# A scan kernel whose tiles hold four channel chunks side by side instead of two, with the products after the scan cut by tokens instead of by chunk pairs

## The chip, the cores and the metric

The kernel runs on one core of a Trainium2 chip. The metric is device time in microseconds (us): the median of several executions. Each profile is one execution, with its own time. The engines are named as in the profile: PE (matmuls and transposes), PEld (its weight loads), ACT (ScalarE), DVE (VectorE), POOL (GpSimd), SP (SyncE, which only issues DMAs here). Every engine works through its own queue in order; semaphores join them.

## The reference: what is computed

The input `x` is 8 x 1024 tokens of 256 features. Three blocks follow each other, each with a residual: half an FP4-quantized gated FFN, a Mamba block, and the same FFN once more.

```
x = x + 0.5 * ffn(layernorm(x))
x = x + mamba(layernorm(x))
x = x + 0.5 * ffn(layernorm(x))
```

The Mamba block is where the change lies. 512 inner channels, 16 states, one recurrence along the tokens for each channel and state:

```
dA = exp(delta[..., None] * A)                    # tokens x 512 x 16
dBu = delta[..., None] * Bm[:, :, None, :] * u[..., None]
h[t] = dA[t] * h[t-1] + dBu[t]
y[t] = sum over states n of h[t, :, n] * Cm[t, n]  ; y = y + u * D
out = (y * silu(z)) @ out_proj_w
```

## The kernel before, in words

The 8192 tokens are cut into 16 chunks of 512 tokens, two to each of the 8 sequences. For a chunk, channels lie on the 128 partitions (four channel chunks, `dc` = 0 to 3) and tokens along the row. Stages: FFN 1 (`stage_f1`), the projections and the convolution (`stage_m1`), the gate z (`stage_z`), the scan over 16 states (`scan`), and the output with FFN 2 (`stage_out`). Several chunks are in work at a time.

**The scan** (`scan_step`, lines 863 to 883). For each state k, ACT makes four tiles `s_bu` (L874) and four tiles `s_da` = exp(delta*A) (L878). PE turns `s_bu` into channel order in PSUM (`s_pb`, L881). DVE runs four scans of 512 tokens (L883), each of which writes one channel chunk into the tile `s_h` (128 x 2048, float32). In chunks that are the first of their sequence, ACT then saves the last token's state (`s_carry`, L908), for the sequence's second chunk; there the scans start from it.

**The layout.** `s_h` is seen through `pairs` (line 528): two halves, each with 512 tokens of two channel chunks that alternate, `(a t q)` with q = 2. So a scan writes every second word of its half. The product with C (`times_c`, L888) runs on POOL in two instructions for each state, one for each half: it multiplies 128 x 1024 elements of `s_h` in place by the row `s_cbc`, in which each value of C is repeated for the two channel chunks of its token (step 0 in the last dimension). In the last chunk's last two states the second of the two runs on DVE.

**The sum over states** is made by DMA: POOL adds each `s_h` to one of two buffers in HBM, `accd` (L920, even and odd states); `accd` starts from u*D, which ACT writes as `m_ud` (L802) in the same layout. At the end of a chunk the buffers are added to the last `s_h` (L914, L915) and POOL multiplies by silu(z) (L852): it reads `s_h` with a step of two words and writes `m_sz`, one instruction for each pair of channel chunks. PE's output projection (L857) follows. In the last chunk the buffers are loaded into `o_y` instead (L835, L836), DVE adds the last two `s_h` (L850) and does the product itself.

**What sets the order.** The program first writes down all instructions, then `set_order` builds a graph of their dependencies, prices them with a table (`price`), searches for a good order on every engine, and pins it. A changed dependency therefore moves instructions everywhere, not just at the place of the edit. `s_h` has five buffers, which `m_ud` and the last chunk's `f_ht` share.

Of the kernel before, what the change touches and what calls it, by code (L numbers as in the profile page):

```python
# [11 lines left out]
F32 = mybir.dt.float32  # L12
BF16 = mybir.dt.bfloat16
I32 = mybir.dt.int32
AF = mybir.ActivationFunctionType
ALU = mybir.AluOpType
# [5 lines left out]
P = 128  # L22
T = 512
# [14 lines left out]
KS = 1  # L38
KE = 1
W_T = ((0.01, 0.08, 0.085), (0.02, 0.09, 0.095), (0.15, 0.25, 0.3), 0.2)  # L40

BE = (0,)
CE = (0,)
BUFS = {
    'accd': 4, 'bcol': 2, 'big': 1, 'bu': 7, 'carry': 2, 'cbc': 2, 'cd': 4, 'da': 4, 'delta': 2,
# [17 lines left out]
ND = DI // P  # L63
# [364 lines left out]
def macaron(ctx: ExitStack, tc: tile.TileContext, x_in, norm_w, norm_b, in_w, conv_w,  # L428
            conv_b, xp_w, dt_w, dt_b, a_log, d_par, out_w, w_gate, w_up, w_down, out):
    nc = tc.nc  # L430
    NB, L, _ = x_in.shape
    chunks = []
    for b in range(NB):
        t = 0
# [23 lines left out]
    dr = ctx.enter_context(tc.tile_pool(name="dr", bufs=3, space=DRAM))  # L458
    sb, psq, psb, dr = Pool(sb), Pool(psq), Pool(psb), Pool(dr)
    pools = [Pool(q) for q in pools]  # L460

    def pst(shape, name):
        turn[kind[0]] += 1
        i = PSM[kind[0]][turn[kind[0]] % len(PSM[kind[0]])]
        t = pools[i].tile([P, 512], F32, tag=f"ps{i}", name=name)
        n = 1
        for k in shape[1:]:
            n *= k
        v = t[: shape[0], :n]
        if len(shape) == 3:  # L470
            v = v.rearrange("p (a b) -> p a b", a=shape[1])
        return v
# [14 lines left out]
    def cload(shape, src, name):  # L487
        t = const.tile(shape, F32, name=name)
        loads.append((t, src))
        return t  # L490
# [3 lines left out]
    def eng(what):  # L494
        return getattr(nc, ENG[what])
# [15 lines left out]
    dh = cload([P, ND], d_par.rearrange("(c p) -> p c", p=P), "dh")  # L511
# [14 lines left out]
        nc.vector.tensor_scalar(an, an, -1.0, None, ALU.mult)  # L526
        yield

    def pairs(h, n):

        return h.rearrange("p (a t q) -> p a t q", a=ND // 2, q=2)[:, :, :n, :]


    def quant(v, n, floor, mul0, mul1):
# [162 lines left out]
    x1d, accd, szd, cd = {}, {}, {}, {}  # L697
    duT, delta, bcol = {}, {}, {}
    carry = {}
# [3 lines left out]
    def tok(ap, s):  # L703
        b, t0, n = chunks[s]
        return ap[b, t0 : t0 + n, :].rearrange("(t p) d -> p t d", p=P)
# [11 lines left out]
    def stage_m1(s):  # L717
        n = chunks[s][2]
        nt = n // P
# [14 lines left out]
        for pr in range(nt // 2):  # L734
# [4 lines left out]
            for j in range(2):  # L739
                t = 2 * pr + j  # L740
                b, r = stats[t]
# [8 lines left out]
        u2 = sb.tile([P, ND, T], F32, tag="big", bufs=BUFS["big"], name="m_u2")  # L750
# [29 lines left out]
        pb = pst([P, nt, P], "m_pb")  # L780
# [12 lines left out]
        nc.scalar.activation(dl, dl, AF.Softplus)  # L793
        yield

        accd[s] = dr.tile([2, P, ND // 2, 2 * T], F32, tag="accd", bufs=BUFS["accd"], name="accd")
        ud = pairs(sb.tile([P, ND * T], F32, tag="h", bufs=BUFS["h"], name="m_ud"), n)
        dg = 1 if fine else DG
        for d0 in range(0, ND, dg):
            d1 = slice(d0, d0 + dg)  # L800
            for dc in range(d0, d0 + dg):
                nc.scalar.activation(ud[:, dc // 2, :, dc % 2], u2[:, dc, :n], AF.Copy, scale=dh[:, dc : dc + 1])  # L802
            eng('du').tensor_tensor(u2[:, d1, :n], u2[:, d1, :n], dl[:, d1], ALU.mult)
        nc.sync.dma_start(accd[s][0], ud.rearrange("p a t q -> p a (t q)"))
        yield
        duT[s] = []
        for t in range(nt):
# [22 lines left out]
    y_of, last_h = {}, {}  # L830

    def load_y(s):
        y = pairs(sb.tile([P, ND * T], F32, tag="big", bufs=BUFS["big"], name="o_y"), chunks[s][2])
        yf = y.rearrange("p a t q -> p a (t q)")
        nc.sync.dma_start(yf, accd[s][0])  # L835
        nc.gpsimd.dma_start(yf, accd[s][1], accum_op=ALU.add)  # L836
        return y

    def stage_out(s):
        n = chunks[s][2]  # L840
        nt = n // P
        muls = (eng('hx'), eng('hq')) if s < S - ENDV else (nc.vector, nc.vector)
        x4 = sb.tile([P, NT, DM], F32, tag="x4", bufs=BUFS["x4"], name="x4b")
        nc.sync.dma_start(x4[:, :nt], x1d[s][:, :nt])
        y, sz = y_of.pop(s), szd[s]

        for a in range(ND // 2):
            if s in last_h:
                for h in last_h[s]:
                    nc.vector.tensor_tensor(y[:, a], y[:, a], h[:, a], ALU.add)  # L850
            zv = sz[:, 2 * a : 2 * a + 2, :]
            (eng('y') if s < S - KE else nc.vector).tensor_tensor(zv, y[:, a].rearrange("p t q -> p q t"), zv, ALU.mult)  # L852
        yield
        for t in range(nt):
            po = pst([P, DM], "o_po")
            for dc in range(ND):
                nc.tensor.matmul(po, sz[:, dc, t * P : (t + 1) * P], outw[:, dc, :], start=(dc == 0), stop=(dc == ND - 1))  # L857
            nc.vector.tensor_tensor(x4[:, t, :], x4[:, t, :], po, ALU.add)
        yield
        yield from ffn(x4, nt, muls, s >= S - KE)  # L860
        nc.sync.dma_start(tok(out, s), x4[:, :nt])

    def scan_step(s, k, h):
        n = chunks[s][2]
        nt = n // P
        first = chunks[s][1] == 0
        bu_v = BE[S - 1 - s] if S - 1 - s < len(BE) else 0
        bu = []
        for t in range(nt):
            b = sb.tile([P, DI], F32, tag="bu", bufs=BUFS["bu"], name="s_bu")  # L870
            if t * bu_v % nt < bu_v:
                nc.vector.tensor_scalar(b, duT[s][t], bcol[s][:, t, k : k + 1], None, ALU.mult)
            else:
                nc.scalar.activation(b, duT[s][t], AF.Copy, scale=bcol[s][:, t, k : k + 1])  # L874
            bu.append(b)
        for dc in range(ND):
            da = sb.tile([P, T], F32, tag="da", bufs=BUFS["da"], name="s_da")[:, :n]
            nc.scalar.activation(da, delta[s][dc], AF.Exp, scale=an[:, dc, k : k + 1])  # L878
            pb = psb.tile([P, T], F32, tag="psb", name="s_pb")[:, :n]
            for t in range(nt):  # L880
                nc.tensor.transpose(pb[:, t * P : (t + 1) * P], bu[t][:, dc * P : (dc + 1) * P], ident)  # L881
            init = 0.0 if first else carry[chunks[s][0]][:, k, dc : dc + 1]
            nc.vector.tensor_tensor_scan(h[:, dc // 2, :, dc % 2], da, pb, init, ALU.mult, ALU.add)  # L883

    def times_c(s, k, h, cbc):
        last = s >= S - KE and k >= NS - 2
        for a in range(ND // 2):
            (nc.vector if last and a else nc.gpsimd).tensor_tensor(  # L888
                h[:, a], h[:, a], cbc.unsqueeze(2).to_broadcast([P, chunks[s][2], 2]), ALU.mult)

    def scan(s):
        n = chunks[s][2]
        if chunks[s][1] == 0:

            carry[chunks[s][0]] = sb.tile([P, NS, ND], F32, tag="carry", bufs=BUFS["carry"], name="s_carry")
        for k in range(0, NS, 2):
            cbc = sb.tile([P, 2, T], F32, tag="cbc", bufs=BUFS["cbc"], name="s_cbc")[:, :, :n]
            nc.sync.dma_start(cbc, cd[s][0:1, k * n : (k + 2) * n].rearrange("o (a t) -> o a t", a=2)
                              .partition_broadcast(P))
            if s >= S - KE and k == NS - 2:  # L900
                y_of[s] = load_y(s)
            last = s >= S - KE and k == NS - 2
            for j in range(2):
                h = pairs(sb.tile([P, ND * T], F32, tag="h", bufs=BUFS["h"], name="s_h"), n)
                hf = h.rearrange("p a t q -> p a (t q)")
                scan_step(s, k + j, h)
                if chunks[s][1] + n < L:
                    nc.scalar.activation(carry[chunks[s][0]][:, k + j].rearrange("p (a q) -> p a q", q=2), h[:, :, n - 1, :], AF.Copy)  # L908
                times_c(s, k + j, h, cbc[:, j, :])
                if last:  # L910
                    last_h.setdefault(s, []).append(h)
                elif k + j == NS - 1:

                    nc.gpsimd.dma_start(hf, accd[s][1], accum_op=ALU.add)  # L914
                    nc.gpsimd.dma_start(hf, accd[s][0], accum_op=ALU.add)  # L915
                    y_of[s] = h
                elif k + j == 1:
                    nc.sync.dma_start(accd[s][1], hf)
                else:
                    nc.gpsimd.dma_start(accd[s][j], hf, accum_op=ALU.add)  # L920
                yield


# [55 lines left out]
```

## Time and profile before

| | us |
|---|---|
| median of three executions | 2452.26 (2449.67 to 2452.42) |
| the profiled execution, its time | 2451.14 |
| its span in the profile | 2449.0 |
| PE busy (clock granted: 0.99 on average) | 2341.7, 96% of the span |
| DVE busy | 2177.9, 89% |
| ACT busy | 2142.2, 87% |
| POOL busy | 2064.2, 84% |

In the profile a busy time is the union of an engine's instructions; matmuls are pipelined and their ends are modelled, so PE's 96% is not PE at its peak. A row of the groups names line, engine, operation, tiles, shapes and count, then busy time and the mean duration of one in ns, then the idle time just ahead of these instructions and what ended most of it. The chain of waits follows the work back from the last instruction, at each step to what released it.

### The profile page before, as it was taken

What the parts mean: (1) busy time and instruction counts of PE and PEld (TensorE: products, weight loads), DVE (VectorE), ACT (ScalarE), POOL (GpSimd) and SP (SyncE); (2) the same over time, 40 slices, a digit from 0 to 9 for tenths busy, and PEclk for the clock granted to TensorE, in tenths of its full rate; (3) what the DMA queues carried; (4) which work ended last, traced back from release to release, by engine and by line L of the source; (5) the groups of instructions that cost most, each with busy time, mean ns of one, the idle gap of its engine ahead of it and who ended that gap; (6) DMA issues with size and microseconds to landing.
All of it is one profiled execution on the core that took longest, in us unless ns stands there. A gap on an engine that the chain in (4) does not pass through costs nothing.

```text
span 2449.0 us, 33713 instructions
## 1 busy us (share of the span) xinstructions
PE 2341.7 (96%) x11260; PEld 1617.9 (66%) x11260; DVE 2177.9 (89%) x3074; ACT 2142.2 (87%) x3952; POOL 2064.2 (84%) x1554
## 2 busy tenths in 40 slices
PE   7989999999999999999999999999999999998888
PEld 5566666667676666666667666666667666655556
DVE  7569898998989899898999889898998989888995
ACT  4489898999989998998999899898998999999852
POOL 4358898899989999898897999899898999888972
PEclk8999999999999999999999999999999999999899
DMA  3049888787877888598886978889787888899970
GB/s 94 18 115 192 192 166 197 166 200 170 165 191 168 203 185 187 138 185 193 175 196 140 210 169 171 189 173 208 167 178 174 179 190 191 189 211 199 198 149 18
DMA packets 90461, 416.28 MB, mean 170 GB/s; under 512 B 12016, under 2 KB 30320, under 8 KB 53552
## 3 DMA queue, kind: packets, MB, share of 16 engines
q0 software_dynamic: 36576, 266.35, 57.6%
q1 hardware_dynamic: 53712, 147.78, 18.4%
q8 instruction: 88, 1.44, 0.2%
q14 instruction: 85, 0.70, 0.1%
HBM read 129.42 MB, written 284.69 MB: 169 GB/s over the span
## 4 chain that ended last, share of the span: by engine, by line
PE 59%; ACT 13%; POOL 11%; DVE 8%; issue 4%; DMA 3%; SPq 0%; POOLq 0%; DVEq 0%; ACTq 0%
PE s_pb L881 11%; PE f_po L662 9%; PE f_pg L642 9%; PE f_pu L642 8%; PE m_pc L765 6%; POOL s_h L888 5%; DVE s_h L883 4%; ACT s_bu L874 4%; PE m_px L755 3%; ACT s_da L878 3%; PE m_pz L823 3%; PE o_po L857 2%; PE m_pp L775 2%; PE m_pd L791 2%; DMA s_h<-accd 2%
## 5 line engine op out<-in xcount | busy, mean ns | idle before, releaser
L888 POOL TENSOR_TENSOR s_h<-s_h,s_cbc 128x1024 f32<-128x1024 f32 x510 | 1136.9, 2270 | 125.0 <-ACT s_carry L908 71.0
L878 ACT ACTIVATE s_da<-m_delta,an 128x512 f32<-128x512 f32 x1024 | 720.7, 718 | 35.3 <-DVE s_h L883 33.5
L881 PEld LDWEIGHTS s_pb<-ident,s_bu 128*128 128x128 f32 x4096 | 505.3, 142 | 335.6 <-issue 132.5
L874 ACT ACTIVATE s_bu<-m_duT,m_bc 128x512 f32<-128x512 f32 x1024 | 701.4, 717 | 12.5 <-PE s_pb L881 9.9
L881 PE MATMUL s_pb<-ident,s_bu 128*128 128x128 f32 x4096 | 652.3, 277 | 44.7 <-DVE s_h L883 34.4
L883 DVE TENSOR_TENSOR_SCAN s_h<-s_da,s_carry,s_pb 128x512 f32<-128x512 f32 x512 | 638.3, 1264 | 22.2 <-PE s_pb L881 18.9
L883 DVE TENSOR_TENSOR_SCAN s_h<-s_da,s_pb 128x512 f32<-128x512 f32 x512 | 608.5, 1206 | 27.3 <-PE s_pb L881 20.2
L662 PE MATMUL f_po<-wdn,f_ht 128*128 128x256 f32 x1536 | 395.3, 382 | 10.0 <-ACT f_ht L659 7.8
L642 PE MATMUL f_pg<-wg,f_xt 128*128 128x352 f32 x1024 | 365.4, 465 | 4.4 <-ACT f_xt L632 1.8
L642 PE MATMUL f_pu<-wu,f_xt 128*128 128x352 f32 x1024 | 360.3, 463 | 5.2 <-DVE f_h L646 3.2
L662 PEld LDWEIGHTS f_po<-wdn,f_ht 128*128 128x128 f32 x1536 | 270.0, 190 | 76.2 <-issue 22.7
L765 PE MATMUL m_pc<-m_xp,cdg 128*128 128x512 f32 x512 | 253.4, 596 | 1.9 <-ACT m_car L762 1.8
L552 POOL TENSOR_TENSOR f_h<-f_h,q_sc 128x704 f32<-128x704 f32 x128 | 195.9, 1534 | 50.8 <-DVE f_h L551 46.2
L642 PEld LDWEIGHTS f_pu<-wu,f_xt 128*128 128x128 f32 x1024 | 177.6, 191 | 89.5 <-issue 21.7
L920 POOL DMA_DIRECT2D accd<-s_h x223 | 209.6, 940 | 26.3 <-POOL s_h L888 18.0
L642 PEld LDWEIGHTS f_pg<-wg,f_xt 128*128 128x128 f32 x1024 | 176.0, 191 | 80.7 <-issue 21.1
L545 POOL TENSOR_TENSOR f_h<-f_h,q_rc 128x704 f32<-128x704 f32 x120 | 176.5, 1479 | 17.0 <-DVE q_rc L544 10.3
L646 DVE SCALAR_TENSOR_TENSOR f_h<-f_h,f_pg 128x352 f32<-128x352 f32 x256 | 129.0, 505 | 37.6 <-ACT f_h L645 36.5
L645 ACT ACTIVATE f_h<-f_pg 128x352 f32<-128x352 f32 x256 | 116.9, 457 | 48.0 <-PE f_pg L642 47.5
L543 POOL TENSOR_SCALAR q_sc<-q_mx 128x44 f32<-128x44 f32 (+2 forms) x198 | 85.5, 439 | 74.2 <-DVE q_mx L542 66.8
L647 DVE TENSOR_TENSOR f_h<-f_h,f_pu 128x352 f32<-128x352 f32 x256 | 129.3, 506 | 18.7 <-PE f_pu L642 17.2
L755 PE MATMUL m_px<-m_hnT,inw 128*128 128x512 f32 x256 | 128.0, 606 | 3.0 <-DVE m_u L769 1.7
(114 smaller groups left out, 3384.6 us busy)
## 6 DMA issues: line engine op xcount, KB each, us to landing
accd<-s_h POOLq DMA_DIRECT2D x223, 1024.0 KB, 9.6
s_cbc<-cd SPq DMA_DIRECT2D x128, 512.0 KB, 6.0
s_h<-accd POOLq DMA_DIRECT2D x30, 1024.0 KB, 8.5
accd<-m_ud SPq DMA_DIRECT2D x16, 1024.0 KB, 13.1
accd<-s_h SPq DMA_DIRECT2D x16, 1024.0 KB, 5.8
x4a<-_attn_hidden_states_dram SPq DMA_DIRECT2D x16, 512.0 KB, 4.3
x1d<-x4a SPq DMA_DIRECT2D x16, 512.0 KB, 6.5
x4b<-x1d SPq DMA_DIRECT2D x16, 512.0 KB, 3.5
```

Source lines behind the costliest of these rows:

```text
L545: mul0.tensor_tensor(vb, vb, rc.unsqueeze(2).to_broadcast([P, g, BLK]), ALU.mult)
L552: mul1.tensor_tensor(vb, vb, sc.unsqueeze(2).to_broadcast([P, g, BLK]), ALU.mult)
L642: nc.tensor.matmul(dst, xt[:, c, :], w[:, c, hf * FH : (hf + 1) * FH], start=(c == 0), stop=(c == 1))
L662: nc.tensor.matmul(po, ht[:, k, :], wdn[:, k, :], start=(k == 0), stop=(k == NF - 1))
L755: nc.tensor.matmul(px, inw[:, c, dc * P : (dc + 1) * P], hnT[:, c, :n], start=(c == 0), stop=(c == 1))
L765: nc.tensor.matmul(pc, cdg[:, dc, k, :], xp[:, k : k + n], start=(k == 0), stop=(k == KC - 1))
L874: nc.scalar.activation(b, duT[s][t], AF.Copy, scale=bcol[s][:, t, k : k + 1])
L878: nc.scalar.activation(da, delta[s][dc], AF.Exp, scale=an[:, dc, k : k + 1])
L881: nc.tensor.transpose(pb[:, t * P : (t + 1) * P], bu[t][:, dc * P : (dc + 1) * P], ident)
L883: nc.vector.tensor_tensor_scan(h[:, dc // 2, :, dc % 2], da, pb, init, ALU.mult, ALU.add)
L888: (nc.vector if last and a else nc.gpsimd).tensor_tensor(h[:, a], h[:, a], cbc.unsqueeze(2).to_broadcast([P, chunks[s][2], 2]), ALU.mult)
L920: nc.gpsimd.dma_start(accd[s][j], hf, accum_op=ALU.add)
```

## The change

`pairs` becomes `mixed`: the tile is `(t q)` with q = 4, so that all four channel chunks alternate and a scan writes every fourth word of the tile. `halves` cuts the 512 tokens into two halves of 256. `times_c` multiplies a half of the tokens at a time, still 128 x 1024 elements, each value of C now repeated four times. The product with silu(z), and the last chunk's additions, go by the same halves: a half reads `s_h` with a step of four words, for 4 x 256 elements. `accd` loses its dimension of pairs; its DMAs move the same bytes. The state for the next chunk is read from four neighbouring words instead of two pairs. `BE` and `CE` go; `BP` is empty, so all `s_bu` stay on ACT as before. The price table is not touched.

```diff
-    def pairs(h, n):
-        return h.rearrange("p (a t q) -> p a t q", a=ND // 2, q=2)[:, :, :n, :]
+    def mixed(h, n):
+        return h.rearrange("p (t q) -> p t q", q=ND)[:, :n, :]
+    def flat(h):
+        return h.rearrange("p t q -> p (t q)")
+    def halves(n):
+        return [slice(0, n // 2), slice(n // 2, n)] if n == T else [slice(0, n)]
...
-        accd[s] = dr.tile([2, P, ND // 2, 2 * T], F32, tag="accd", bufs=BUFS["accd"], name="accd")
-        ud = pairs(sb.tile([P, ND * T], F32, tag="h", bufs=BUFS["h"], name="m_ud"), n)
+        accd[s] = dr.tile([2, P, ND * T], F32, tag="accd", bufs=BUFS["accd"], name="accd")
+        ud = mixed(sb.tile([P, ND * T], F32, tag="h", bufs=BUFS["h"], name="m_ud"), n)
...
-                nc.scalar.activation(ud[:, dc // 2, :, dc % 2], u2[:, dc, :n], AF.Copy, scale=dh[:, dc : dc + 1])
+                nc.scalar.activation(ud[:, :, dc], u2[:, dc, :n], AF.Copy, scale=dh[:, dc : dc + 1])
...
-        for a in range(ND // 2):
+        for a in halves(n):
             if s in last_h:
                 for h in last_h[s]:
                     nc.vector.tensor_tensor(y[:, a], y[:, a], h[:, a], ALU.add)
-            zv = sz[:, 2 * a : 2 * a + 2, :]
+            zv = sz[:, :, a]
             (eng('y') if s < S - KE else nc.vector).tensor_tensor(zv, y[:, a].rearrange("p t q -> p q t"), zv, ALU.mult)
...
-            nc.vector.tensor_tensor_scan(h[:, dc // 2, :, dc % 2], da, pb, init, ALU.mult, ALU.add)
+            nc.vector.tensor_tensor_scan(h[:, :, dc], da, pb, init, ALU.mult, ALU.add)
 
     def times_c(s, k, h, cbc):
         last = s >= S - KE and k >= NS - 2
-        for a in range(ND // 2):
-            (nc.vector if last and a else nc.gpsimd).tensor_tensor(
-                h[:, a], h[:, a], cbc.unsqueeze(2).to_broadcast([P, chunks[s][2], 2]), ALU.mult)
+        for a in halves(chunks[s][2]):
+            m = a.stop - a.start
+            (nc.vector if last and not a.start else nc.gpsimd).tensor_tensor(
+                h[:, a], h[:, a], cbc[:, a].unsqueeze(2).to_broadcast([P, m, ND]), ALU.mult)
...
-                h = pairs(sb.tile([P, ND * T], F32, tag="h", bufs=BUFS["h"], name="s_h"), n)
-                hf = h.rearrange("p a t q -> p a (t q)")
+                h = mixed(sb.tile([P, ND * T], F32, tag="h", bufs=BUFS["h"], name="s_h"), n)
                 scan_step(s, k + j, h)
                 if chunks[s][1] + n < L:
-                    nc.scalar.activation(carry[chunks[s][0]][:, k + j].rearrange("p (a q) -> p a q", q=2), h[:, :, n - 1, :], AF.Copy)
+                    nc.scalar.activation(carry[chunks[s][0]][:, k + j], h[:, n - 1, :], AF.Copy)
                 times_c(s, k + j, h, cbc[:, j, :])
```

More of the change, by code (lines that the diff above doesn't have):

```diff
@@ L40 @@
 W_T = ((0.01, 0.08, 0.085), (0.02, 0.09, 0.095), (0.15, 0.25, 0.3), 0.2)
-BE = (0,)
-CE = (0,)
+BP = ()
 BUFS = {
@@ L801, in stage_m1 @@
             for dc in range(d0, d0 + dg):
-                nc.scalar.activation(ud[:, dc // 2, :, dc % 2], u2[:, dc, :n], AF.Copy, scale=dh[:, dc : dc + 1])
+                nc.scalar.activation(ud[:, :, dc], u2[:, dc, :n], AF.Copy, scale=dh[:, dc : dc + 1])
             eng('du').tensor_tensor(u2[:, d1, :n], u2[:, d1, :n], dl[:, d1], ALU.mult)
-        nc.sync.dma_start(accd[s][0], ud.rearrange("p a t q -> p a (t q)"))
+        nc.sync.dma_start(accd[s][0, :, : ND * n], flat(ud))
         yield
@@ L832, in load_y @@
     def load_y(s):
[L833 to L836, printed above, removed]
+        n = chunks[s][2]
+        y = mixed(sb.tile([P, ND * T], F32, tag="big", bufs=BUFS["big"], name="o_y"), n)
+        nc.sync.dma_start(flat(y), accd[s][0, :, : ND * n])
+        nc.gpsimd.dma_start(flat(y), accd[s][1, :, : ND * n], accum_op=ALU.add)
         return y
@@ L866, in scan_step @@
         first = chunks[s][1] == 0
-        bu_v = BE[S - 1 - s] if S - 1 - s < len(BE) else 0
         bu = []
@@ L870, in scan_step @@
             b = sb.tile([P, DI], F32, tag="bu", bufs=BUFS["bu"], name="s_bu")
-            if t * bu_v % nt < bu_v:
-                nc.vector.tensor_scalar(b, duT[s][t], bcol[s][:, t, k : k + 1], None, ALU.mult)
+            if s < S - KE and (k, t) in BP:
+                nc.gpsimd.tensor_scalar(b, duT[s][t], bcol[s][:, t, k : k + 1], None, ALU.mult)
             else:
@@ L912, in scan @@
                 elif k + j == NS - 1:
-                    nc.gpsimd.dma_start(hf, accd[s][1], accum_op=ALU.add)
-                    nc.gpsimd.dma_start(hf, accd[s][0], accum_op=ALU.add)
+                    nc.gpsimd.dma_start(flat(h), accd[s][1, :, : ND * n], accum_op=ALU.add)
+                    nc.gpsimd.dma_start(flat(h), accd[s][0, :, : ND * n], accum_op=ALU.add)
                     y_of[s] = h
                 elif k + j == 1:
-                    nc.sync.dma_start(accd[s][1], hf)
+                    nc.sync.dma_start(accd[s][1, :, : ND * n], flat(h))
                 else:
-                    nc.gpsimd.dma_start(accd[s][j], hf, accum_op=ALU.add)
+                    nc.gpsimd.dma_start(accd[s][j, :, : ND * n], flat(h), accum_op=ALU.add)
                 yield
```

## The prediction

> **What bounds the kernel now.** I read the engine totals and the chain of waits first, then the busy times by stretch, then the rows of the lines that the edit touches.
>
> ```profile
> span 2449.0 us, 33713 instructions
> ...
> PE 2341.7 (96%) x11260; PEld 1617.9 (66%) x11260; DVE 2177.9 (89%) x3074; ACT 2142.2 (87%) x3952; POOL 2064.2 (84%) x1554
> ...
> PE 59%; ACT 13%; POOL 11%; DVE 8%; issue 4%; DMA 3%; SPq 0%; POOLq 0%; DVEq 0%; ACTq 0%
> PE s_pb L881 11%; PE f_po L662 9%; PE f_pg L642 9%; PE f_pu L642 8%; PE m_pc L765 6%; POOL s_h L888 5%; DVE s_h L883 4%; ACT s_bu L874 4%; PE m_px L755 3%; ACT s_da L878 3%; PE m_pz L823 3%; PE o_po L857 2%; PE m_pp L775 2%; PE m_pd L791 2%; DMA s_h<-accd 2%
> ```
>
> No engine stands alone: the chain lies 59% on PE, and the other three are busy 84 to 89%. The same in the middle, by stretches (PE, PEld, DVE, ACT, POOL busy us with counts, granted clock, DMA):
>
> ```profile
> 1050.00:1200.00 150.00, 146.63 (x705) 100.65 (x704) 136.47 (x188) 137.36 (x255) 139.37 (x104) 0.99 0.87 191
> ...
> 1500.00:1650.00 150.00, 147.83 (x724) 103.30 (x723) 140.97 (x207) 139.24 (x262) 134.01 (x101) 1.00 0.78 173
> ```
>
> Of 150 us DVE is busy 136 to 141, ACT 137 to 139, POOL 134 to 139. So a saving on POOL alone comes through in part, while a price laid on DVE finds only 9 to 14 us of idle time in each such stretch. The clock is full. Now the rows (minimum/median/maximum ns) of the products, and what they wait for:
>
> ```profile
> L888 POOL TENSOR_TENSOR s_h<-s_h,s_cbc x510: 2120/2147/3019, 154.7 to 2368.1; 128x1024 f32<-128x1024 f32 x170
> ...
>   ACT s_carry L908: 71.0, 53
>   DVE s_h L883: 48.8, 67
> ```
>
> ```profile
> L803 POOL TENSOR_TENSOR m_u<-m_u,m_delta x34: 1271/2371/3002, 137.3 to 2250.7; 128x1024 f32<-128x1024 f32 x30, 128x512 f32<-128x512 f32 x4
> ```
>
> ```profile
> L545 POOL TENSOR_TENSOR f_h<-f_h,q_rc x120: 1375/1388/2262, 90.1 to 2372.4; 128x704 f32<-128x704 f32 x120
> ...
> L545 POOL TENSOR_TENSOR f_xn<-f_xn,q_rc x64: 1047/1062/1362, 23.9 to 2411.3; 128x512 f32<-128x512 f32 x64
> ```
>
> **The products with C (L888).** POOL's product gets cheaper the longer its second operand stands still. With a new value at every element (L803) 128x1024 takes 2371 ns; with each value used twice (L888) 2147. Used 16 times (L545) 704 elements take 1388 and 512 take 1062: 1.70 ns per element, so 1024 would take 1388 + 320 x 1.70 = 1932. Against the share of new values: from 1 to 1/2 224 ns, from 1/2 to 1/16 215 ns. On the second line a share of 1/4 gives 2147 - 215 x (0.25/0.4375) = 2024, that is 118 to 123 ns less; I take 118. 510 x 0.118 = 60 us less of POOL. What of it reaches the end: L888 holds 5.0% of the chain, 122 us, of 1137 busy, so 0.107 us for each us. 60 x 0.107 = **-6.4 us**. Bounds: 0 if POOL's work is hidden everywhere; at most about -30, because with POOL out of the way PE, 147 of 150 us, leaves 2 us for each of the 15 dense stretches.
>
> **What the products wait for.** The order of the two programs shows it. Before, a chunk that saves its state makes the first product wait for ACT's `s_carry` (127 of 254 tiles), since the saved token lies in both halves. Afterwards no first product waits for ACT; the second does, and the first (2 us) covers it. The wait for ACT was 71.0/53 = 1.34 us a time, that for scans alone 48.8/67 = 0.73; the difference over 53 is 32 us of POOL's idle time. Against it, in the other chunks a first product could start after two scans and now needs all four: 2 x 1.27 = 2.5 us later for each of 127 tiles, 317 us in all, most of it filled from POOL's queue; at POOL's idle share of 16%, 50 us. At 0.107 these are -3.4 and +5.4, the bounds; as only 67 waits for scans were seen in all, I take **-1**. Queued behind a waiting product on POOL are the next tile's product and the FFN's quantization (L545, L552), for which DVE and ACT wait; behind the DMA that adds the tile to `accd` (9.6 us to land) stands its buffer, one of five, each held about 25 us at one tile per 9.6 us, so there is room.
>
> **The scans (L883), the unknown.** They wrote every second word and now write every fourth. No row has a step of four words.
>
> ```profile
> L883 DVE TENSOR_TENSOR_SCAN s_h<-s_da,s_pb x512: 1158/1211/1223, 149.5 to 2241.0; 128x512 f32<-128x512 f32 x171
> L883 DVE TENSOR_TENSOR_SCAN s_h<-s_da,s_carry,s_pb x512: 1174/1272/1282, 278.9 to 2372.2; 128x512 f32<-128x512 f32 x171
> ```
>
> ```profile
> L802 ACT ACTIVATE m_ud<-m_u,dh x64: 738/765/817, 93.3 to 2239.1; 128x512 f32<-128x512 f32 x64
> ```
>
> ```profile
> L874 ACT ACTIVATE s_bu<-m_duT,m_bc x1024: 699/713/772, 143.8 to 2360.1; 128x512 f32<-128x512 f32 x171
> ```
>
> A DVE operation of one pass takes 672 ns on 512 elements (L827); the scan takes 1211, two passes, some 2.1 ns per element, so a write has two slots of time. What a step costs shows on ACT: the same operation, dense 713 (L874), with a step of two words 765 (L802): 52 ns, 0.10 per element on top of 0.84 (704 against 512 elements at L549: 162/192). Read as a pace, 0.94 ns for two words walked over, four words take 1.88, under the scan's 2.1: hidden, 0. Read as a charge, 52 ns for each doubling that nothing hides, two doublings make 104: 1024 x 0.104 = 107 us of DVE. Lower bound 0 (the arithmetic doesn't change). I take **0**, by the nearest row on DVE itself: L852 in the last chunk reads with a step of two words in 1220 ns, and L850, dense, takes 1220 too, so at one pass per element DVE shows no charge.
>
> [...]
>
> **Silu(z) (L852, 30 on POOL)** reads with a step of four words instead of two: 2421 ns now. Nearest row: its 50 ns over the dense L803, once more: 30 x 0.05 = 1.5 us, at 0.107 **+0.2**. Dear end: ACT's pace, 0.94 more per element, 29 us, +3.1. [...]
>
> **m_ud (L802, 64 on ACT)** writes with four: 52 ns again, 3.3 us; at ACT's 13% of the chain over its 2142 busy (0.15) **+0.5**. Dear end, the pace: 31 us, +4.6. DMAs: the same 1024 KB each, rows stay whole: 0.
>
> **The end.** DVE's four additions (L850) start at 2379.78, when `o_y` has landed (issued at 2371.47, 8.1 us). Afterwards half the tokens are ready after two additions and a product instead of four and two, 3.5 us sooner for PE; but in the new order two quantization steps (0.88 each) and an eviction stand between them, and the eviction of the first output tile still stands behind both halves. **-0.5**, bounds -2.2 and +2.
>
> **Sum:** -6.4 - 1 + 0 + 0.2 + 0.5 - 0.5 = -7.2 on 2451.14 (span 2449.0 and 2.1 around it), which gives 2444. The median lies 1.1 above the profiled execution, inside the spread, so I leave it.
>
> **Rivals.**
> 1. *The scans pay for their step* (slower). Place: L883; price 104 ns, 107 us of DVE. For it: DVE idles only 9 to 14 us in 150; 107/15 = 7 us in each stretch fill most of that, and ACT and PE wait for DVE's scans (33.5, 34.4 and 95.8 us). At the chain's rate for L883 (4.2%, 103 us, of 1247 busy: 0.08) it costs 9 us, with nothing hidden 107; I take half, 54 - 7 = 47: **2498**. At half, 14 ns per scan eat the sum of 7.2 us, and 24 ns make the kernel measurably slower; from there it decides. Against it: two passes per element, and L852 on DVE. 0.30.
> 2. *The wait for all four scans costs more than the product saves* (mildly slower): +5.4 and the dear ends +3.1 and +4.6, the end's +2, against -6.4, together +8.7: **2460**. For it: 127 first products lose their early start. Against: POOL has other work queued. 0.12.
> 3. *The change doesn't do what it says*: POOL's gain ends at two uses, or all of it is hidden (59% of the chain is PE): **2452**. For it: POOL is the least busy engine. Against: the row at 16 uses. 0.15.
>
> **Numbers.** Forecast, scans unchanged and a cheaper product: 0.43, 2444, its own range 2420 (the -30) to 2451. About 0.2%, 4.9 us, is what a measurement of this kernel can tell from no change; so faster 0.43, same 0.15, slower 0.42. The likeliest case lies on one side, but cases of both signs hold the chance; the range 2420 to 2540 reaches into the first rival's upper half and leaves out its dear end (2550) and the page's.
>
> **What would show it.** Right: L888's successor near 2030 ns, scans still 1211 and 1272, POOL's wait for `s_carry` gone, POOL near 2005 busy. Wrong: scans above 1260 and 1320 with DVE over 2230 busy (rival 1); scans as before and POOL's wait for scans over 90 us (rival 2); the product at 2147 (rival 3). The forecast also fails if the new order alone moves the time by more than the few us summed here.

## The result, and the profile after

The changed kernel is slower: median 2476.51 us of four executions (2471.53 to 2477.18) against 2451.39 of the kernel before beside it. The ratio is 1.0099, its 95% interval 1.0081 to 1.0116: **25 us lost** where 7 were forecast as a gain. The profiled execution took 2476.16 us.

The page of the changed kernel, its span, engine totals and chain of waits:

```profile
span 2474.3 us, 33739 instructions
...
PE 2341.7 (95%) x11260; PEld 1622.3 (66%) x11260; DVE 2187.2 (88%) x3074; ACT 2158.1 (87%) x3952; POOL 2016.3 (81%) x1554
...
PE 39%; ACT 20%; POOL 17%; DVE 10%; DMA 7%; issue 7%; POOLq 0%; SPq 0%; ACTq 0%; DVEq 0%
POOL s_h L892 7%; PE s_pb L884 7%; PE f_pg L646 6%; PE f_pu L646 6%; ACT s_bu L877 5%; ACT s_da L881 5%; DVE s_h L886 5%; PE m_pc L769 5%; PE f_po L666 5%; DMA s_h<-accd 3%; PE m_px L759 2%; DMA accd<-s_h 2%; PE m_pz L827 2%; PE o_po L861 2%; POOL m_sz L856 2%
```

POOL has 48 us less to do (2064.2 before), as meant. PE's work is the same to a tenth of a microsecond. ACT has 16 us more, and the chain has moved off PE: 39% instead of 59%, with ACT and POOL at 20% and 17%. A kernel with less work in sum that takes longer has lost the time to waiting. The two dense stretches of the prediction show it (PE, PEld, DVE, ACT, POOL):

```profile
1050.00:1200.00 150.00, 142.84 (x699) 99.53 (x698) 134.79 (x192) 137.71 (x255) 132.54 (x102) 1.00 0.87 191
1500.00:1650.00 150.00, 147.77 (x716) 101.98 (x715) 138.98 (x191) 138.61 (x255) 131.91 (x101) 1.00 0.83 178
```

In the first, PE and POOL idle some 4 and 7 us longer (POOL in part because its products are shorter); ACT, with 137.7, is as busy as before. The rows that answer to those of the prediction, with the same columns, first the product and what it waits for:

```profile
L892 POOL TENSOR_TENSOR s_h<-s_h,s_cbc x510: 1991/2024/3307, 156.2 to 2389.3; 128x1024 f32<-128x1024 f32 x170
...
  DVE s_h L886: 141.0, 93
...
  ACT s_carry L911: 9.9, 11
```

2024 ns is the predicted number. The wait for `s_carry` has all but gone (9.9 us of 71.0), and the wait for scans has grown from 48.8 to 141.0, over the 90 us that the prediction named as the mark of rival 2. The scans:

```profile
L886 DVE TENSOR_TENSOR_SCAN s_h<-s_da,s_pb x512: 1158/1215/1259, 150.2 to 2260.9; 128x512 f32<-128x512 f32 x171
L886 DVE TENSOR_TENSOR_SCAN s_h<-s_da,s_carry,s_pb x512: 1178/1273/1305, 274.7 to 2388.0; 128x512 f32<-128x512 f32 x171
```

4 ns and 1 ns more in the median, 6 and 5 in the mean (1206 to 1212, 1264 to 1269): rival 1 falls. The two groups that the prediction all but left out, first `m_ud`, then silu(z):

```profile
L806 ACT ACTIVATE m_ud<-m_u,dh x64: 1204/1245/1278, 93.3 to 2243.5; 128x512 f32<-128x512 f32 x64
```

```profile
L856 POOL TENSOR_TENSOR m_sz<-s_h,m_sz x30: 2882/2972/3542, 300.1 to 2292.0; 128x1024 f32<-128x1024 f32 x30
...
L856 DVE TENSOR_TENSOR m_sz<-o_y,m_sz x2: 1954/1986/2017, 2400.1 to 2405.8; 128x1024 f32<-128x1024 f32 x2
```

Silu(z) before, on both engines:

```profile
L852 POOL TENSOR_TENSOR m_sz<-s_h,m_sz x30: 2405/2421/2617, 288.3 to 2277.9; 128x1024 f32<-128x1024 f32 x30
L852 DVE TENSOR_TENSOR m_sz<-o_y,m_sz x2: 1218/1220/1221, 2384.3 to 2385.5; 128x1024 f32<-128x1024 f32 x2
```

`m_ud` went from 765 to 1245 ns, silu from 2421 to 2972 on POOL and from 1220 to 1986 on DVE. These are 480, 551 and 766 ns; the prediction had given the first two 52 and 50.

Where along the span the time goes shows in the moment at which each chunk's first scan starts. After minus before it is -4.3 us for chunk 1, 3.4 for chunk 5, -4.3 for chunk 9, 3.9 for chunk 13, then 21.1 for chunk 14 and 8.7 for chunk 15; the last scan ends 16 us later, the span 25. So in this plan most of the loss lies behind 2000 us. One part of it is the end itself, on DVE (start, us, operation, wait ahead of it), first before, then after:

```profile
2379.78 4.62 DVE L850 TENSOR_TENSOR o_y<-o_y,s_h 128x1024 f32<-128x1024 f32 x4
...
2389.19 0.85 DVE L858 TENSOR_TENSOR x4b<-x4b,o_po 128x256 f32<-128x256 f32 x2 [2.18 <-PE o_po L857]
```

```profile
2396.18 1.23 DVE L854 TENSOR_TENSOR o_y<-o_y,s_h 128x1024 f32<-128x1024 f32 x1 [2.37 <-DMA o_y<-accd]
2397.32 0.88 DVE L554 SCALAR_TENSOR_TENSOR f_h<-q_q,f_h 128x704 f32<-128x704 f32 x1
2398.12 1.22 DVE L854 TENSOR_TENSOR o_y<-o_y,s_h 128x1024 f32<-128x1024 f32 x1
2399.26 0.88 DVE L555 SCALAR_TENSOR_TENSOR f_h<-q_q,f_h 128x704 f32<-128x704 f32 x1
2400.06 1.95 DVE L856 TENSOR_TENSOR m_sz<-o_y,m_sz 128x1024 f32<-128x1024 f32 x1
2401.93 2.37 DVE L854 TENSOR_TENSOR o_y<-o_y,s_h 128x1024 f32<-128x1024 f32 x1
...
2405.80 2.02 DVE L856 TENSOR_TENSOR m_sz<-o_y,m_sz 128x1024 f32<-128x1024 f32 x1
2410.63 0.42 DVE L667 SCALAR_TENSOR_TENSOR x4b<-f_po,x4b 128x256 f32<-128x256 f32 x1 [2.82 <-PE f_po L666]
2413.44 0.85 DVE L862 TENSOR_TENSOR x4b<-x4b,o_po 128x256 f32<-128x256 f32 x2 [2.39 <-PE o_po L861]
```

From `o_y`'s landing to the first output eviction (L862) pass 17.2 us, where before it was 9.4 (2379.78 to 2389.19). By their durations the dear products with silu are 1.5 us of these 8. But run 1, in the same order and without the dear steps, takes 17.6 us for the same stretch (2385.20 to 2402.80), so the stretch is long by the order of DVE's queue: quantization steps and evictions stand between the additions, and one addition takes 2.37 us.

Three theories stood after this. **S**: the two operations that walk `s_h` in steps of four words cost the time. **W**: the wait of the first product for all four scans costs it. **O**: a changed graph gives another plan, and the plan as such costs it.

### The profile page after: what moved, and what is told of

Its sections match the earlier page's. It is cut to its first block, busy times and chain, and to the rows that moved or that the text cites. A ratio compares the mean times of both kernels' runs of the same rounds, so it can differ in the third digit from the quotient of the medians.

```text
span 2474.3 us, 33739 instructions
## 1 busy us (share of the span) xinstructions
PE 2341.7 (95%) x11260; PEld 1622.3 (66%) x11260; DVE 2187.2 (88%) x3074; ACT 2158.1 (87%) x3952; POOL 2016.3 (81%) x1554
## 4 chain that ended last, share of the span: by engine, by line
PE 39%; ACT 20%; POOL 17%; DVE 10%; DMA 7%; issue 7%; POOLq 0%; SPq 0%; ACTq 0%; DVEq 0%
POOL s_h L892 7%; PE s_pb L884 7%; PE f_pg L646 6%; PE f_pu L646 6%; ACT s_bu L877 5%; ACT s_da L881 5%; DVE s_h L886 5%; PE m_pc L769 5%; PE f_po L666 5%; DMA s_h<-accd 3%; PE m_px L759 2%; DMA accd<-s_h 2%; PE m_pz L827 2%; PE o_po L861 2%; POOL m_sz L856 2%
## 5 line engine op out<-in xcount | busy, mean ns | idle before, releaser
L892 POOL TENSOR_TENSOR s_h<-s_h,s_cbc 128x1024 f32<-128x1024 f32 x510 | 1069.5, 2159 | 162.3 <-DVE s_h L886 141.0
L884 PEld LDWEIGHTS s_pb<-ident,s_bu 128*128 128x128 f32 x4096 | 510.6, 142 | 330.1 <-issue 131.7
L884 PE MATMUL s_pb<-ident,s_bu 128*128 128x128 f32 x4096 | 664.9, 277 | 52.4 <-DVE s_h L886 42.9
L886 DVE TENSOR_TENSOR_SCAN s_h<-s_da,s_carry,s_pb 128x512 f32<-128x512 f32 x512 | 643.7, 1269 | 29.8 <-PE s_pb L884 25.7
L886 DVE TENSOR_TENSOR_SCAN s_h<-s_da,s_pb 128x512 f32<-128x512 f32 x512 | 614.3, 1212 | 29.6 <-PE s_pb L884 21.9
L923 POOL DMA_DIRECT2D accd<-s_h x223 | 215.4, 966 | 29.1 <-POOL s_h L892 14.2
L549 POOL TENSOR_TENSOR f_h<-f_h,q_rc 128x704 f32<-128x704 f32 x120 | 183.5, 1530 | 13.3 <-DVE q_rc L548 8.8
L861 PE MATMUL o_po<-outw,m_sz 128*128 128x256 f32 x512 | 126.4, 383 | 13.2 <-POOL m_sz L856 6.9
```

What stands on the lines that cost most here:

```text
L549: mul0.tensor_tensor(vb, vb, rc.unsqueeze(2).to_broadcast([P, g, BLK]), ALU.mult)
L886: nc.vector.tensor_tensor_scan(h[:, :, dc], da, pb, init, ALU.mult, ALU.add)
L892: (nc.vector if last and not a.start else nc.gpsimd).tensor_tensor(h[:, a], h[:, a], cbc[:, a].unsqueeze(2).to_broadcast([P, m, ND]), ALU. ...
L923: nc.gpsimd.dma_start(accd[s][j, :, : ND * n], flat(h), accum_op=ALU.add)
```

## The experiments

Two kinds of kernel were run. In one the order of instructions on every engine is *pinned*: written into the kernel as a list, so that only durations change. In the other the planner makes a new plan. Runs 1, 5 to 7, 9 and 10 are pinned; in their traces the operations of PE, ACT, DVE and POOL follow each other as in the kernel whose order they take. Ratios are to the kernel before beside each run.

**1. After's own order, without the dear steps.** Theory S in the order of the changed kernel.

```diff
-                nc.scalar.activation(ud[:, :, dc], u2[:, dc, :n], AF.Copy, scale=dh[:, dc : dc + 1])
+                nc.scalar.activation(flat(ud)[:, dc * n : (dc + 1) * n], u2[:, dc, :n], AF.Copy, scale=dh[:, dc : dc + 1])
...
-    ...tensor_tensor(zv, y[:, a].rearrange("p t q -> p q t"), zv, ALU.mult)
+    ...tensor_tensor(zv, flat(y[:, a]).rearrange("p (q t) -> p q t", q=ND), zv, ALU.mult)
```

> The changed kernel in its own order, instruction by instruction, but ACT writes u*D densely into m_ud and the product with silu(z) reads y densely (the elements land in the wrong places; only the time is read). Theory S (the operations with a step of four words make the loss: 64 on ACT at +0.48 us, 30 on POOL at +0.55, 2 on DVE at +0.77): the time falls to 2451 to 2457. Theory W (the first product waits for all four scans): 2470 to 2476. Theory O (the new order as such): 2468 to 2476.

2459.28 us, ratio 1.0035 (1.0023 to 1.0047): 17 of the 25 us come back. The product's waits in this kernel, and the two groups that became cheap, `m_ud` and silu(z):

```profile
  DVE s_h L863: 143.4, 92
...
  ACT s_carry L888: 11.6, 12
```

```profile
L783 ACT ACTIVATE m_ud<-m_u,dh x64: 704/712/739, 93.2 to 2233.0; 128x512 f32<-128x512 f32 x64
```

```profile
L833 POOL TENSOR_TENSOR m_sz<-s_h,m_sz x30: 2352/2386/2975, 300.2 to 2280.5; 128x1024 f32<-128x1024 f32 x30
```

The wait for scans stays at 143 us, and the time is all but back. So W falls as the main cause. The chunks now run ahead of before's (chunk 9 by 9.0 us, chunk 13 by 3.1); chunk 14 starts 11.7 late, but chunk 15 is 2.2 early again. The loss at the end stays: from the end of the last scan to the end of the span it is 84.7 us here, 85.1 in the changed kernel and 75.7 before. (This profiled execution took 2465.43, 6 us above the median.)

**2. The old layout, cut by tokens.** Two words, but products and silu by halves of the tokens, so that the wait for four scans is there without the step.

```diff
... (the product with silu(z) and the last chunk's additions in the same way)
-        for a in range(ND // 2):
-            (nc.vector if last and a else nc.gpsimd).tensor_tensor(
-                h[:, a], h[:, a], cbc.unsqueeze(2).to_broadcast([P, chunks[s][2], 2]), ALU.mult)
...
+        for a in (slice(0, n // 2), slice(n // 2, n)):
+            c = cbc[:, a].unsqueeze(2).to_broadcast([P, n // 2, 2])
+            c = c.unsqueeze(1).to_broadcast([P, 2, n // 2, 2])
+            (nc.vector if last and not a.start else nc.gpsimd).tensor_tensor(h[:, :, a], h[:, :, a], c, ALU.mult)
```

> The kernel before with its layout of two words, but the products with C and with silu(z) go by halves of the tokens: the wait for all four scans without the step of four words; a product with C stays at 2147 ns, silu(z) at 2421, m_ud at 765. Theory W: 2470 to 2480 (POOL's wait for scans goes up to some 140 us as in the changed kernel, and POOL keeps its 60 us). Theory S: 2448 to 2456. Theory O: the order is planned anew, anywhere from 2445 to 2475.

2469.55, ratio 1.0075 (1.0057 to 1.0092): slower by 18 with the old prices of all operations. The product's waits:

```profile
  DVE s_h L883: 70.5, 61
  ACT s_carry L910: 3.0, 2
```

The wait for scans grows to 70.5 us only, not to the 140 that were expected, and both waits together are less than before's (48.8 and 71.0). The loss could still be W or O; run 7 decides.

**3. The new layout, product by channel pairs.** Steps of four, but a first product needs two scans only.

```diff
-        for a in halves(chunks[s][2]):
-            m = a.stop - a.start
-            (nc.vector if last and not a.start else nc.gpsimd).tensor_tensor(
-                h[:, a], h[:, a], cbc[:, a].unsqueeze(2).to_broadcast([P, m, ND]), ALU.mult)
+        for a in range(ND // 2):
+            v = h[:, :, 2 * a : 2 * a + 2]
+            (nc.vector if last and a else nc.gpsimd).tensor_tensor(
+                v, v, cbc.unsqueeze(2).to_broadcast([P, chunks[s][2], 2]), ALU.mult)
```

> The changed layout of four words and all else as changed, but the product with C goes by pairs of channel chunks (runs of two words, then a hop of two), so that a first product may start after two scans again. Theory W: 2450 to 2460, unless the product itself gets dearer by its hops. Theory S: 2472 to 2480, since m_ud and silu(z) keep their dear steps. Theory O: anywhere from 2450 to 2480.

2482.23, ratio 1.0123 (1.0108 to 1.0138). The waits are back as they were, and the kernel is no faster than the changed one:

```profile
L892 POOL TENSOR_TENSOR s_h<-s_h,s_cbc x510: 2122/2183/3104, 157.8 to 2399.2; 128x1024 f32<-128x1024 f32 x170
...
  ACT s_carry L911: 64.2, 46
  DVE s_h L886: 16.8, 16
```

The wait for scans is gone (141 to 17 us) and nothing is gained. That speaks against W, but not by itself: the product is dearer again (2183 ns instead of 2024), the wait for `s_carry` is back, and the plan is new.

**4. The last chunk in the old layout**, all others in the new (`s_h`, `m_ud`, `o_y` and the products of chunk 15 as before).

```diff
+    def lay(h, s):
+        if s >= S - KE:
+            return h.rearrange("p (a t q) -> p a t q", a=ND // 2, q=2)[:, :, :n, :]
+        return mixed(h, n)
```

> The changed kernel, but the last of the 16 chunks keeps the layout and the products of before. Whatever the mechanism, it tells the place: if the loss lies in the last chunk (the scans of chunk 13 begin at 2001 us before and 2004 us after, so 21 of the 25 us come later than that), the time falls to 2452 to 2460. If it lies in chunks before the last, 2470 to 2477.

2471.13, ratio 1.0077 (1.006 to 1.0093): 5 of the 25 us go with the last chunk's layout, not the whole. The plan is new, so these 5 alone would lie inside the scatter of plans (runs 11 to 18). The traces say the same, though: from the end of the last scan to the end of the span it is 77.7 us here, against 85.1 in the changed kernel and 75.7 before.

**5. Before's order, with the cheap product alone.** Pinned; each row of C is read in runs of four.

```diff
-                h[:, a], h[:, a], cbc.unsqueeze(2).to_broadcast([P, chunks[s][2], 2]), ALU.mult)
+                h[:, a].rearrange("p (t r) q -> p t (r q)", r=2), h[:, a].rearrange("p (t r) q -> p t (r q)", r=2),
+                cbc[:, : chunks[s][2] // 2].unsqueeze(2).to_broadcast([P, chunks[s][2] // 2, 4]), ALU.mult)
```

> The kernel before in its own order, instruction by instruction, but each product with C reads a row in which a value is used four times (the first 256 values of C for all 512 tokens, so the numbers are wrong; only the time is read): POOL's 2147 ns become 2024 and nothing else changes. If the products' cheaper price reaches the end as the first three experiments add up (18 us for the halves, 17 for the dear steps, 25 in all, so -10 for the products): 2439 to 2443. If it is hidden behind the other engines: 2449 to 2452. At the chain's rate of 0.107: 2445.

2447.55, ratio 0.9974 (0.9964 to 0.9984): 6.2 us faster. The product and POOL's total in this kernel:

```profile
L865 POOL TENSOR_TENSOR s_h<-s_h,s_cbc x510: 1999/2022/2615, 154.6 to 2361.9; 128x1024 f32<-128x1024 f32 x170
```

```profile
PE 2342.6 (96%) x11260; PEld 1621.8 (66%) x11260; DVE 2175.5 (89%) x3074; ACT 2144.4 (88%) x3952; POOL 2004.7 (82%) x1554
```

POOL does 60 us less, and 6.2 reach the end: 0.10 us for each. The prediction had -6.4.

**6. Before's order, with the dear steps alone.** Pinned; `m_ud` is written and the tile of the silu product read with a step of four words.

```diff
-    ...activation(ud[:, dc // 2, :, dc % 2], u2[:, dc, :n], AF.Copy, ...)
+    ...activation(udf[:, dc : 4 * n : 4], u2[:, dc, :n], AF.Copy, ...)
...
-    ...tensor_tensor(zv, y[:, a].rearrange("p t q -> p q t"), zv, ALU.mult)
+    ...tensor_tensor(zv.rearrange("p q (b t) -> p (q b) t", b=2), y[:, a].rearrange("p t q -> p (t q)").rearrange("p (t r) -> p r t", r=4), zv.rearrange("p q (b t) -> p (q b) t", b=2), ALU.mult)
```

> The kernel before in its own order, but ACT writes m_ud with a step of four words and the product with silu(z) reads y with a step of four (elements land and come from the wrong places; only the time is read): m_ud 765 to 1245 ns, silu(z) 2421 to 2970 on POOL and 1220 to 1990 on DVE. Theory S: +15 to +18 here too, 2466 to 2470. If the dear steps hurt only in the changed kernel's order: 2452 to 2457.

2474.93, ratio 1.0088 (1.0074 to 1.0102): 21 us slower, in an order that hasn't moved. The two groups:

```profile
L780 ACT ACTIVATE m_ud<-m_u,dh x64: 1181/1242/1286, 92.8 to 2259.6; 128x512 f32<-128x512 f32 x64
```

```profile
L830 POOL TENSOR_TENSOR m_sz<-s_h,m_sz x30: 2861/2922/3076, 288.1 to 2299.2; 128x1024 f32<-128x1024 f32 x30
```

Here the loss is even: the start of a chunk's first scan falls back by 5.9 us at chunk 5, 11.3 at chunk 9, 17.7 at chunk 13 and 20.8 at chunk 15, about 1.3 for each chunk.

**7. Before's work, in the order of run 2.** Pinned, nothing else changed: a first product again needs two scans only, the order stays.

> The kernel before, its work untouched, in the order that was planned for the token halves in the layout of two words (e2), where a first product may run as soon as two scans are done but its place in POOL's queue is the later one. Theory O (the order as such costs e2's 18 us): 2465 to 2471. Theory W (waiting for all four scans costs it): 2451 to 2457.

2471.67, ratio 1.0072 (1.0058 to 1.0086), against 2469.55 in run 2. The waits:

```profile
  ACT s_carry L885: 51.0, 30
  DVE s_h L860: 4.0, 5
```

The wait for scans has gone, that for `s_carry` is back, and the time stays. In this order the cut by tokens costs nothing; the order by itself, with before's work, costs 18.

**8. The changed kernel with a true price table.** The planner's table charges the product by the length of the run (how often each value of C is repeated), so it knew of the saving; it charged `m_ud` and silu as ever.

```diff
         hold = n / 1.2 + (51 if psum else 93) + 93 * sum(size(a) == 1 for a in ins[1:])
+        hold += 480 * (n == T and dims(outs[0])[-1][0] == ND)
...
+        if kind == "InstTensorTensor" and dims(ins[0])[-1][0] == ND:
+            return n * 1.79 + 69, 0, 0, True
...
+        if dims(ins[0])[-1][0] == ND:
+            return n * 2.64 + 165, 0, 0, port
```

> The changed kernel with the planner's price table mended: m_ud +0.48 us, silu(z) +0.55 on POOL and +0.75 on DVE, so that the order is planned with the durations that the trace shows. If the dear steps hurt because the plan didn't know them: 2458 to 2466. If they hurt by their work alone, or the loss is the waits': 2472 to 2480.

2456.51, ratio 1.0005 (0.9994 to 1.0015): 20 us come back, with every operation as dear as in the changed kernel:

```profile
L811 ACT ACTIVATE m_ud<-m_u,dh x64: 1198/1246/1287, 94.2 to 2233.8; 128x512 f32<-128x512 f32 x64
```

```profile
L861 POOL TENSOR_TENSOR m_sz<-s_h,m_sz x30: 2884/2960/3564, 296.4 to 2270.9; 128x1024 f32<-128x1024 f32 x30
```

```profile
L897 POOL TENSOR_TENSOR s_h<-s_h,s_cbc x510: 1994/2027/2922, 159.0 to 2365.6; 128x1024 f32<-128x1024 f32 x170
...
  DVE s_h L891: 127.2, 92
```

The wait for scans is 127 us in a kernel as fast as before's: another sign against W. Is what came back due to knowledge of the prices, or to a lucky plan? Runs 11 to 15, 17 and 18 ask that.

**9 and 10. The two dear operations one at a time**, in before's order, by one of run 6's two edits each.

> The kernel before in its own order; of the two dear steps only m_ud's write (ACT, 64 times 765 to 1245 ns, 31 us) is kept, elements land in the wrong places. If each us on ACT counts as in the both-steps run (21 us for 31 on ACT and 17 on POOL, 0.44 each): 2465. If ACT alone is what hurts: 2470 to 2474. If POOL's is: 2452 to 2457.

`m_ud` alone: 2463.91, ratio 1.0053 (1.0036 to 1.007), 13 us for 64 x 0.48 = 31 us of ACT, 0.43 for each. Its row, and all that waited for it:

```profile
L780 ACT ACTIVATE m_ud<-m_u,dh x64: 1204/1241/1282, 93.2 to 2250.3; 128x512 f32<-128x512 f32 x64
...
  PEld s_pb L859: 0.5, 2
```

Next to nothing waits for `m_ud` itself. That it costs by holding up what follows it on ACT is likely, but which of that work carries the 13 us the rows don't show.

> The same with silu(z)'s read alone (POOL, 30 times 2421 to 2930 ns, 15 us, and 2 on DVE at +0.75 us). If each us counts alike: 2460. If ACT alone hurts: 2452 to 2456. If POOL's: 2468 to 2474.

Silu alone: 2461.42, ratio 1.0045 (1.0028 to 1.0061), 11 us for 30 x 0.51 = 15 us of POOL and 1.5 of DVE, two thirds of it:

```profile
L829 POOL TENSOR_TENSOR m_sz<-s_h,m_sz x30: 2860/2930/3142, 287.8 to 2285.2; 128x1024 f32<-128x1024 f32 x30
```

Together the two give 24, where run 6 gave 21. Who waits for silu explains its high rate. Before, then in run 10:

```profile
  PEld o_po L857: 4.9, 10
  PE o_po L857: 0.8, 2
```

```profile
  PEld o_po L834: 18.3, 25
  PE o_po L834: 8.6, 16
```

The output projection stands right behind the product, and PE's waits for it grow by some 21 us (the two rows can overlap, so at most that).

**11 to 18. What plans differ by.** Run 11 is the changed kernel with other random draws where the planner chooses among its plans. The other runs plan anew with other weights of its search, one set (0.04, 0.08, 0.12, 0.18, 0.25) in runs 12 to 14, another (0.06, 0.12, 0.18, 0.24, 0.35) in runs 15, 17 and 18; the kernel's own are (0.05, 0.1, 0.15, 0.2, 0.3).

```diff
-random.Random(k)
+random.Random(k + 100)
```

```diff
-WEIGHTS = (0.05, 0.1, 0.15, 0.2, 0.3)
+WEIGHTS = (0.04, 0.08, 0.12, 0.18, 0.25)
```

Run 11, the changed kernel, other draws:

> The changed kernel, price table as it was, but the planner draws other random delays when it picks among its plans, and so picks another. It shows how far the order alone moves the changed kernel. If the 20 us that the mended prices gave back came from knowing the prices: 2470 to 2482, near the changed kernel. If they were the luck of another plan: it may be anywhere from 2452 to 2476.

Run 12, before, first other weights:

> The kernel before, its work untouched, planned with other weights (0.04, 0.08, 0.12, 0.18, 0.25) at the start of the planner's search, so with another order. If the order of before was nothing special: 2449 to 2456. If orders differ by chance as much as the token halves' order showed (18 us): 2460 to 2475.

Run 13, the changed kernel, first other weights:

> The changed kernel, price table as it was, planned with the weights of e12. If the mended prices gave back 20 us by being true: 2470 to 2485, like the two unmended plans so far (2476, 2479). If by luck: as likely as not 2455 to 2465.

Run 14, true prices, first other weights:

> The changed kernel with the mended prices, planned with the weights of e12. If knowing the prices helps: 2450 to 2466. If e8 was luck: 2466 to 2482.

Run 15, true prices, second other weights:

> The changed kernel with the mended prices and a third set of weights (0.06, 0.12, 0.18, 0.24, 0.35). If knowing the prices helps: 2450 to 2466. If e8 was luck: 2466 to 2482.

Run 17, before, second other weights:

> The kernel before, planned with the third set of weights of e15. With 2451 and 2465 (e12) it makes the third plan of the kernel before, to set beside three mended plans of the changed one (2457, 2454, 2468, mean 2460). If the change, planned with true prices, is worth its products (6 us): 2466 to 2480, so that the mean of before lies above 2460. If it is worth nothing: about 2460.

Run 18, the changed kernel, second other weights:

> The changed kernel, price table as it was, with the third set of weights: the partner of e15 and e17. If true prices help: 2475 to 2490. If not: 2455 to 2470.

| weights | before | changed | changed, true prices |
|---|---|---|---|
| the kernel's own | 2451.4 | 2476.5 | 2456.5 (run 8) |
| first other set | 2464.6 (run 12) | 2486.7 (run 13) | 2453.5 (run 14) |
| second other set | 2479.6 (run 17) | 2482.9 (run 18) | 2468.4 (run 15) |

Run 11 took 2478.82, ratio 1.0114 (1.0098 to 1.0129). Read down a column: the same work in another plan differs by up to 28 us. Read along a row: the true table beats the untouched one each time, by 20, 33 and 14.5, and the four plans of the changed kernel (2476.5 to 2486.7) lie above all three with true prices (2453.5 to 2468.4). Seven plans would fall apart like that by chance in 1 of 35 cases (the ways to pick three of seven). That speaks clearly for the prices; how much of one pair's difference is luck is not shown.

Run 16 tried for a version better than both: true prices, and `s_bu` of two states on POOL to relieve ACT.

```diff
-BP = ()
+BP = ((4, 0), (10, 0))
```

> The changed kernel with the mended prices, and states 4 and 10 make their first s_bu on POOL instead of ACT in all chunks but the last (the switch BP, empty in the change): 30 instructions of 0.72 us leave ACT, about the 31 us that m_ud's dear step adds there, and POOL gets 30, some 25 to 30 us, half of what its products gave back. If ACT's extra work is what is left of the loss: 2440 to 2449, below both kernels. If the plan decides: anywhere from 2448 to 2470.

2480.48, ratio 1.012 (1.0105 to 1.0135). One plan of one such kernel, 24 us above run 8, inside the scatter of plans (up to 28 us for the same work); it says nothing firm about the idea. As a fourth plan with true prices, though of other work, it lies among those without them. No version that does the whole computation beat the kernel before.

Two tests are missing: the changed work in the old order, and the old work in the changed order.

## Why the prediction was wrong, point by point

- **The products, -6.4: right.** 2024 ns as predicted, and -6.2 measured with everything else held still (run 5; by its interval 4 to 9), with POOL at 2004.7 busy there. The price of the product was reasoned from rows. The rate (0.107 from the chain's share) was not: the same rule missed the other two rates below by three and six times, so that it fits here may be luck.
- **The scans, 0: right.** The step of four words costs them 4 and 1 ns in the median. The prediction's reason, two passes per element that hide it, was its author's estimate, read from 1211 ns for a scan against 672 for L827; no run shows it. The range of 2420 to 2540 leaves out two dear ends of the scans, 2550 and another whose price no run shows; in place of both the runs showed 1215 and 1273 ns for a scan.
- **The waits, -1, and rival 2: the wait was there, its price was not.** The row named as the mark of rival 2 (POOL's wait for scans over 90 us) appeared with 141: 92 us more, where the prediction allowed 50, against 61 less for `s_carry`, where it counted 32. The clean tests are run 1 (17 us faster with 143 us of the wait, in the same order) and run 7 (its absence gains nothing in run 2's order). Runs 3 and 8 agree, in new plans. Here a big wait (141 us, in run 1 143) on an engine with slack (POOL, busy 81% of the span) cost nothing that shows.
- **`m_ud`, +0.5, and silu(z), +0.2: here the prediction failed.** It took the nearest row's 50 ns, once more, for a step twice as long, and pushed the other ends into rival 2. Measured: 480 ns and 501 to 551 ns, 13 and 11 us. Two errors lie in this. First, size. The pace that the prediction worked out for ACT (1.88 ns for each element at four words) was trusted to argue that the scans hide it, but for `m_ud` and silu it was only the dear end. By it `m_ud` costs 31 us of ACT, which it did. A reading that is trusted for one term has to be applied to the other terms. For silu the surcharge is 0.54 ns per element (551 over 1024), between the 0.05 that was taken and the 0.94 of the dear end. Second, the rate. The dear ends were turned into time by the chain's shares, 0.15 and 0.107, and gave 4.6 and 3.1; measured rates are 0.43 and about 0.67. A chain share is an average over all of an engine's work. The products' 510 small savings came through at that average (0.10). Silu's 30 additions of 0.5 us stand right ahead of PE's output projection and came through at six times of it; why `m_ud`'s come through at three times of theirs stays open.
- **The new order, priced at nothing: the second failure.** The prediction said that it fails "if the new order alone moves the time by more than the few us summed here", and left that out of its sum and range. Plans of the same work differ by 10 to 28 us (the range of each column), run 2's order costs 18 with before's work unchanged (run 7), and before's own plan is the fastest of its three. The edit also made the table untrue in two rows: the planner made room for a cheaper product, and none for two dearer operations.
- **The end, -0.5, at worst +2: wrong in sign and size.** 8 us from `o_y` to the first eviction are lost, not gained, in run 1 as well, so not by the dear steps. From the end of the last scan to the end of the span every plan with the new layout in the last chunk takes 79.5 to 85.2 us (changed kernel, runs 1, 3, 8, 11, 13 to 16, 18), before's plans and run 4 take 75.7 to 78.6 (before, runs 4, 5, 6, 9, 10, 12, 17); in runs 2 and 7 it is 80.2 and 79.4. The prediction saw the quantization steps that stand between the additions, and took them for nearly free.

What makes up the 25 us? In before's order: 21 for the dear steps (run 6), less 6 for the products (run 5), which leaves some 10 for the order and all else that the edit moved. In after's order: 17 for the dear steps (run 1), and +8 left for the order and the products together. That is as much as the end loses (8 us up to the first eviction), but that the products give their 6 in after's order too is not shown. So the dear steps are the larger part in both (17 to 24 us by runs 1, 6, 9 and 10), and the split between them and the order stays open by that much. Where they are known to the planner, much of them is hidden (run 8), in part perhaps by that plan's luck. The mean over three plans is 2459.5 with true prices and 2465.2 before; with columns that scatter by 15 and 28 us, this difference decides nothing.

## What to carry to other kernels

When a layout is changed for one operation, list every operation that reads or writes the tile, and price each at the new step by the pace of its own engine (here a step of four words for two added 480 ns to ACT's `m_ud`, 551 to POOL's silu(z), 766 to DVE's, and 4 and 1 to DVE's scans); a rare one can count much for each microsecond where another engine waits right behind it (silu(z), 32 times, about 0.67; the products, 510 times, 0.10). In a kernel whose order a planner makes from a price table, a change of layout is a change of that table, and an edit's worth is known only from several plans on each side, or from a pinned order in which one duration is changed at a time.

## What the runs showed of the hardware that was not expected

- A step of four float32 words costs next to nothing in one place and much in another. DVE's scan writes with it at 1215 ns against 1211 at two words. DVE's product with silu(z) reads with it at 1986 ns against 1220 at two words for 1024 elements, 0.75 ns more for each, though 1220 is also what an addition takes that reads densely (L850, before).
- On ACT a write with a step of one, two and four words takes 712 (run 1, `m_ud`), 765 and 1245 ns for 512 elements: nearly flat, then steep.
- POOL's product with a held second operand goes 2371 (L803, before), 2147 (L888, before), 2024 ns (L892, the changed kernel) for 1024 elements as each value stands for 1, 2 and 4 elements; the gain (224, then 123) nearly halves with the second doubling.
